# Half pages for the last rows of experts, in a two-layer graph network with routed experts

## The chip, the cores and the metric

The kernel runs on one core of a Trainium2 chip. The metric is device time in microseconds for one execution, on that core. Its engines are TensorE (PE; PEld is its weight load), VectorE (DVE), ScalarE (ACT), GpSimd (POOL) and SyncE (SP). Transfers are issued from the queues of SP, ACT and POOL and run on 16 DMA engines.

## What is computed

128 graphs of 64 nodes, so N = 8192 rows of D = 256 values in fp32, go through two layers. Each layer is a graph step and then a mixture of experts; both add to x.

```python
# layer 0
x = x + gnn0(layernorm(x), adj)      # (adj @ x + eps * x) W1, rmsnorm, silu, W2
h = layernorm(x)
logits = h @ gate_w.T                # 64 experts
top, idx = top_k(logits, 6)          # softmax over the 6
mix = sum_k softmax(top)[k] * (h @ lattice_weights[idx[k]])   # 256 x 256 each
x = x + layernorm(h + mix @ out_w.T + out_b)
# layer 1
h = layernorm(layernorm(x))          # the second one has gamma and beta
x = x + relu-conv(h, adj, W_rel, W_root)
h = layernorm(x)
top, idx = top_k(h @ Wg + bg, 2)     # 8 experts, softmax over the 2
x = x + sum_k softmax(top)[k] * (relu(h @ W1[e] + b1[e]) @ W2[e] + b2[e])
```

A row so goes to 6 of 64 experts in layer 0 (49152 copies) and to 2 of 8 in layer 1 (16384 copies). Which experts is known only while the kernel runs.

## The kernel before

**Routing.** Both layers use the class Router. Row blocks of 256 are scored; each chosen copy gets a place in a table in DRAM (`r0x`, `r1x`), in its expert's part of it, and POOL writes it there with one indirect DMA per 128 copies (`send`, L408). A copy carries its destination and its gate value in two extra columns (W = D + 2). Behind the last copy of each expert, ACT's queue writes a filler page whose destination lies outside the answers (`fill_end`, L519 to L525).

An expert's copies are read back in pages: 128 rows in layer 0 (pg = P), 256 in layer 1 (pg = 2 P). Its last page may be partly filled; in layer 0 each of 64 experts can have one. `page_table` (L432 to L517), a long row of small DVE operations at the end of the routing, orders all pages: first the full pages up to R per expert, then the other full ones, then the partly filled ones. For page number i the table `tab` gives the row where it begins (row 0 of `tab`) and its expert (row 1). SP loads the row number into a register before it fetches a page, PE loads the expert's number before its matmuls. The number of pages that the data needs, `total_pages`, is compared with a static number by `needed`: pages beyond it stand inside `tc.If` and run only if needed.

**Layer 0's experts.** The weights of all 64 experts lie in SBUF (`lat`). 12 early pages, one for each of 12 experts, are taken first (`fetch_early`, `flip_early`, `apply_early`). Then pages run in pairs: `fetch` (SP, L554, one DMA a page into `px`, 22 buffers of a pair), `flip` (four PE transposes into PSUM, one ACT copy to `pxT`), `apply` (two matmuls a page, L1068, then a DVE scaling by the gate value, L1072), and `reply`: POOL's indirect DMA that scatters 128 answers into `r0y` (L415). `staggered` writes the order out: at step s, the fetch of pair s + 12, `apply` of pair s, and the flip of pair s + 3 (s + 2 for the first four).

**The fused pass.** It runs over 32 blocks: `load_y` (L1197) fetches the six answers of each row, `mixture` sums them with transposes, `out_proj`, layer norm, then layer 1's graph step with `w_rel` and `w_root`, and layer 1's routing. Answers for the first 6 blocks (READY) are known to come from pages in the front of the order, so these loads need not wait for the last replies; later ones do. The small weights are asked for on ACT's queue as the pass begins (L1182 to L1186). The order of engines' instructions is written by hand here too.

**Layer 1's experts.** Four first pages (FIRST, numbers -4 to -1; three of them are fetched within the fused pass) and then pages 0 to 64. `fetch1` brings a page's rows into `px` (4 buffers), the expert's first weights into `pw` (3 buffers, 514 KB) and its bias into `pb`; `flip1` transposes, `up` makes the hidden values (16 matmul records over 256 columns, ACT's relu), `down` multiplies by the second weights (16 records), `share` makes the gate value, and `answer` (L1169 to L1175) adds the bias and scales on DVE into `py_s` (2 buffers) and has POOL add the rows to the output in DRAM: `add` (L423 to L430), one accumulating indirect DMA per 128 rows, two a page. The adds of one page need not wait for each other, but those of the next page wait until these have landed, as two pages can hold the same row.

`answer(-4)` and `answer(-3)` stand in DVE's order behind layer 1's `page_table` (L1486 to L1493).

Of the kernel before, what the change touches and what calls it, by code (L numbers as in the profile page):

```python
# [106 lines left out]
class Router:  # L107
# [15 lines left out]
    def __init__(self, tc, pool, small, dram, n, D, E, K, T, pg, S, epoch, name, R, total=None, like=None):  # L123
# [4 lines left out]
        self.pages = K * n // pg + E - 1  # L128

        self.likely_pages = K * n // pg + E // 2 + max(E // 8, 1)  # L130
# [301 lines left out]
    def page_table(self, scratch):  # L432
# [28 lines left out]
        v.scalar_tensor_tensor(part, full, -float(pg), cnt, op0=ALU.mult, op1=ALU.add)  # L461
        v.tensor_scalar(part, part, 0.0, None, op0=ALU.is_gt)
# [5 lines left out]
        self.total_pages = self.pool.tile([P, 1], I32, name=n + "total")  # L468
        if self.seen is None:
            v.tensor_copy(self.total_pages, cum[:, V - 1:V])  # L470
        else:

            far = small([1], "far")
            v.scalar_tensor_tensor(cnt, first, -float(pg), self.seen, op0=ALU.mult, op1=ALU.add)
            if self.taken is not None:
                v.scalar_tensor_tensor(cnt, self.taken, -float(pg), cnt, op0=ALU.mult, op1=ALU.add)
            v.tensor_reduce(far, cnt, op=ALU.max, axis=AX.X)
            v.tensor_scalar(far, far, 0.0, float(self.pages), op0=ALU.is_gt, op1=ALU.mult)
            v.tensor_tensor(self.total_pages, far, cum[:, V - 1:V], op=ALU.max)
# [4 lines left out]
        self.tab = self.pool.tile([P, 2, 4], I32, name=n + "tab")  # L484
# [32 lines left out]
        v.tensor_scalar(self.tab[:, 1, :], exp, float(E - 1), None, op0=ALU.min)  # L517

# [8 lines left out]
    def load(self, what, i, engine):  # L527

        top = (self.spare, self.E - 1)[what]
        _, v = self.nc.values_load_multi_w_load_instructions(  # L530
            self.tab[i // 4:i // 4 + 1, what, :], engines=[engine], min_val=0, max_val=top,
            skip_runtime_bounds_check_because="the page table holds no other values for any counts")
        return v
# [14 lines left out]
    def fetch_first(self, row, out):  # L548

        d = self.nc.sync.dma_start(out=out, in_=self.table[ds(row, self.pg), :].rearrange("(t p) d -> p t d", p=P))  # L550
        self.tc.declare_no_dep(d.ins, group=self.name + "late", reason="full pages get no rows")

# [16 lines left out]
def two_layer_gnn_moe_kernel(ctx: ExitStack, tc: tile.TileContext, a: dict, out: bass.AP):  # L569
# [16 lines left out]
    READY = 6  # L586
    FOLD = 2
# [88 lines left out]
    with tc.tile_pool(name="c0", bufs=1) as c0, \  # L676
# [201 lines left out]
        r0 = Router(tc, const, small, dram, N, D, E0, K0, T, P, 14 * P, 4, "r0", 3)  # L878
        r1 = Router(tc, const, small, dram, N, D, E1, 2, T, 2 * P, N, 4, "r1", 1, total=out, like=r0)
# [136 lines left out]
    with tc.tile_pool(name="wx0", bufs=3, reuse_waits="tile") as wx, \  # L1016
# [3 lines left out]
        pairs = [dict() for _ in range(npair)]  # L1020
# [16 lines left out]
        def fetch(j):  # L1037
            Q = pairs[j]
            Q["px"] = px = wx.tile([P, 2, W], F32, name="px", bufs=22)
            for q in range(2):  # L1040
                i = 2 * j + q
                if i % 4 == 0:
                    regs["row"] = r0.load(0, i, ENG.SP)
                if i < r0.pages:
                    r0.fetch(i, regs["row"][i % 4], px[:, q:q + 1, :])

        def flip(j):
            Q = pairs[j]
            pt = pt_pool.tile([P, KD, C], F32, name="pt")
            n = min(2, r0.pages - 2 * j)  # L1050
# [3 lines left out]
            Q["xT"] = xT = ring.pop() if ring else wx.tile([P, KD, C], F32, name="pxT", bufs=5)  # L1054
            nc.scalar.copy(xT[:, :, :n * P], pt[:, :, :n * P])  # L1055

        def apply(j):
# [3 lines left out]
            if j % 2 == 0:  # L1061
                regs["e"] = r0.load(1, 2 * j, ENG.PE)
            py = py_pool.tile([P, 2, D], F32, name="py")
            px, xT = Q["px"], Q["xT"]
            n = min(2, r0.pages - 2 * j)
            for q in range(n):
                for k in range(KD):
                    nc.tensor.matmul(py[:, q, :], lhsT=xT[:, k, ts(q, P)],  # L1068
                                     rhs=lat[:, ds(regs["e"][(2 * j + q) % 4], 1), k, :].rearrange("p o d -> p (o d)"),
                                     start=(k == 0), stop=(k == KD - 1))  # L1070
            for q in range(n):
# [5 lines left out]
                  (-2, lambda j: flip(j) if j < 4 else None), (-3, lambda j: flip(j) if j >= 4 else None))  # L1077
        likely = (r0.likely_pages - EARLY + 3) // 4 * 2

        mean_pages = (K0 * N // P + E0 // 2 - EARLY) // 4 * 2  # L1080
        staggered(mean_pages, (*stages, (0, load_vectors)))
        wait = const.tile([1, 4], F32, name="wait")
        with tc.If(r0.needed(2 * mean_pages)):
            staggered(likely, stages, mean_pages)
            with tc.If(r0.needed(2 * likely)):
                staggered(npair, stages, likely)
# [11 lines left out]
    FIRST = 4  # L1098
    pages = {i: dict() for i in range(-FIRST, r1.pages)}
    regs = {}  # L1100

    likely = r1.likely_pages - FIRST

# [7 lines left out]
    def fetch1(i):  # L1111
        Q = pages[i]
        Q["x"] = x = wx.tile([P, 2, W], F32, name="px", bufs=4)
# [6 lines left out]
        if i % 4 == 0 or i == likely:  # L1120
            regs["row"], regs["esp"] = r1.load(0, i, ENG.SP), r1.load(1, i, ENG.SP)
        r1.fetch(i, regs["row"][i % 4], x)
        load1(i, regs["esp"][i % 4])


    def flip1(i):
        Q = pages[i]
        pt = Q["pt"](0)
        ops.transpose(pt, Q["x"])
        Q["xT"] = xT = wx.tile([P, KD, PG], F32, name="pxT")  # L1130
        nc.scalar.copy(xT, pt)

    def up(i, lo=0, hi=KF):
        Q = pages[i]
        w = Q["w"]
# [3 lines left out]
        for c0 in range(lo, hi, Q["group"]):  # L1139
            group = range(c0, c0 + Q["group"])  # L1140
            ph = [Q["ph"](c) for c in group]
            for c in group:
                for k in range(KD):
                    nc.tensor.matmul(ph[c - c0], lhsT=w[:, k * F1 + c * P:k * F1 + (c + 1) * P],  # L1144
                                     rhs=Q["xT"][:, k, :], start=(k == 0), stop=(k == KD - 1))
            for c in group:
                nc.scalar.activation(hid[:, c, :], ph[c - c0], AF.Relu, bias=w[:, KD * F1 + c:KD * F1 + c + 1],  # L1147
                                     scale=1.0)

    def down(i, e, tiles=(0, 1)):  # L1150
        Q = pages[i]
        if 0 in tiles:
# [8 lines left out]
    def share(i):  # L1161

        Q = pages[i]
        Q["p"] = p = wx.tile([P, 2], F32, name="p")
        nc.scalar.activation(p, Q["x"][:, :, D + 1], AF.Exp)  # L1165
# [3 lines left out]
    def answer(i):  # L1169
        Q = pages[i]  # L1170
        y, p = wx.tile([P, 2, D], F32, name="py_s"), Q["p"]
        nc.vector.tensor_add(y, Q["py"], Q["b2"].unsqueeze(1).to_broadcast([P, 2, D]))  # L1172
        for t in range(2):
# [3 lines left out]
    with tc.tile_pool(name="c3", bufs=1, reuse_waits="tile") as c3, \  # L1177
# [6 lines left out]
        w_rel = load_matrix(c3, "L1_gnn_W_rel")  # L1184
        w_root = load_matrix(c3, "L1_gnn_W_root")
# [7 lines left out]
        def load_y(b):  # L1193
            B = blocks[b]
            B["y"] = y = work.tile([P, T, K0, D], F32, name="y", bufs=3)
            for t in range(T):
                d = nc.sync.dma_start(out=y[:, t],  # L1197
                                      in_=r0.answer[ts(b * T + t, P * K0), :].rearrange("(p k) d -> p k d", k=K0))
                if b < READY:
                    tc.declare_no_dep(d.ins, group="r0last", reason="in the first pages, or waited for above")  # L1200

# [212 lines left out]
        for i in (-4, -3, -2):  # L1414
# [3 lines left out]
            (-2, load3),  # L1418
            (-4, load_y),
# [76 lines left out]
    with tc.tile_pool(name="pt4", bufs=2, space=PSUM, reuse_waits="tile") as pt_pool, \  # L1496
# [7 lines left out]
        def finish(i):  # L1504
            if 0 <= i < E1:
                r1.fill_end(i)
            if i >= 0 and (i % 4 == 0 or i == likely):
                regs["e"] = r1.load(1, i, ENG.PE)
            share(i)
            down(i, regs["e"][i % 4] if i >= 0 else i + FIRST)  # L1510
# [10 lines left out]
        stages = (-2, fetch), (0, then(flip1)), (1, finish), (0, then(up))  # L1521
        staggered(likely, stages, -2)
        with tc.If(r1.needed(likely)):
            staggered(r1.pages, stages, likely)
# [32 lines left out]
```

## Time and profile before

| What | us |
|---|---|
| median of 3 runs (1998.88 to 2004.12) | 1999.45 |
| the profiled execution | 2002.07 |
| its span, first to last instruction | 2000.2 |
| PE busy | 1879.9 (94%) |
| POOL busy | 1160.2 (58%) |
| DVE busy | 1150.2 (58%) |
| ACT busy | 1010.0 (50%) |

The page of the profile gives the busy time of each engine, then the span in 40 slices of 50 us with the busy share in tenths, the granted clock of PE (PEclk), and the DMA share. Groups of instructions follow: line, engine, operation, what is written and read, count, then busy time, the mean of one in ns, the idle time before them and what ended it. A matmul in fp32 shows as two records. The trace can also be asked for the busy time in a stretch, for waits (who waited for whom: total, times, longest), for the timeline of an engine (start, length, what), and for the chain of work that ended last. A line number can be that of a helper: L415 is every reply, L425 every add.

### The profile page before, as it was taken

What the parts mean: (1) busy time and instruction counts of PE and PEld (TensorE: products, weight loads), DVE (VectorE), ACT (ScalarE), POOL (GpSimd) and SP (SyncE); (2) the same over time, 40 slices, a digit from 0 to 9 for tenths busy, and PEclk for the clock granted to TensorE, in tenths of its full rate; (3) what the DMA queues carried; (4) which work ended last, traced back from release to release, by engine and by line L of the source; (5) the groups of instructions that cost most, each with busy time, mean ns of one, the idle gap of its engine ahead of it and who ended that gap; (6) DMA issues with size and microseconds to landing.
All of it is one profiled execution on the core that took longest, in us unless ns stands there. A gap on an engine that the chain in (4) does not pass through costs nothing. (4 is left out here: it accounts for less than half of the span.)

```text
span 2000.2 us, 36067 instructions
## 1 busy us (share of the span) xinstructions
PE 1879.9 (94%) x10004; PEld 1628.7 (81%) x10004; DVE 1150.2 (58%) x4231; ACT 1010.0 (50%) x2033; POOL 1160.2 (58%) x1134
## 2 busy tenths in 40 slices
PE   7999999999947899999999799999999999999996
PEld 6888888888836778888777688888788888888885
DVE  5899999999974333444333489999842222222221
ACT  5888888888821222222222366666733333333331
POOL 1377777777777777777777744444453434444343
PEclk9999999999978999999999999999999999999998
DMA  4234555554468988666665799787247666666674
GB/s 127 72 127 137 161 163 163 161 163 132 153 220 271 288 259 255 208 206 207 212 205 167 283 380 336 263 282 257 96 131 184 160 150 152 160 163 161 152 167 88
DMA packets 265148, 381.07 MB, mean 191 GB/s; under 512 B 55000, under 2 KB 218984, under 8 KB 264944
## 3 DMA queue, kind: packets, MB, share of 16 engines
q1 hardware_dynamic: 185744, 230.88, 38.8%
q0 software_dynamic: 64416, 136.14, 22.5%
q10 hardware_dynamic: 14784, 11.64, 1.8%
q8 instruction: 90, 1.47, 0.3%
q14 instruction: 114, 0.93, 0.2%
HBM read 214.45 MB, written 168.25 MB: 191 GB/s over the span
## 5 line engine op out<-in xcount | busy, mean ns | idle before, releaser
L408 POOL DMA_INDIRECT r0x<-xs,r0row x384 | 386.9, 1008 | 216.9 <-ACT lat L784 114.3
L415 POOL DMA_INDIRECT r0y<-px x404 | 392.8, 972 | 124.6 <-DMA r0y<-px 49.4
L1068 PE MATMUL py<-lat,pxT 128*128 x1616 | 389.6, 385 | 17.1 <-ACT pxT L1055 13.8
L425 POOL DMA_INDIRECT out_x<-py_s,px x138 | 214.5, 1554 | 303.6 <-DMA out_x<-py_s,px 256.5
L1072 DVE TENSOR_SCALAR px<-py,px 128x256 f32<-128x256 f32 x404 | 177.0, 479 | 310.3 <-PE py L1068 304.6
L1068 PEld LDWEIGHTS py<-lat,pxT 128*128 128x128 f32 x1616 | 294.0, 192 | 57.0 <-ACT pxT L1055 18.2
L1055 ACT COPY pxT<-pt 128x512 f32<-128x512 f32 x202 | 117.9, 585 | 369.4 <-PE pt L1053 251.6
L1147 ACT ACTIVATE phid<-ph,pw 128x256 f32<-128x256 f32 x264 | 125.0, 473 | 312.0 <-PE ph L1144 232.6
L1157 PE MATMUL py<-fw,phid 128*128 (+1 forms) x1072 | 243.2, 380 | 1.3 <-issue 0.6
L795 PE MATMUL ps<-lat 128*128 128x256 f32 x1024 | 238.9, 382 | 0.0
L1144 PE MATMUL ph<-pxT,pw 128*128 128x256 f32 x1056 | 238.7, 379 | 0.0
L759 PE MATMUL ph<-lat 128*128 128x256 f32 x1024 | 232.5, 386 | 3.2 <-DVE lat L782 2.0
L408 POOL DMA_INDIRECT r1x<-xs,r1row x128 | 135.6, 1059 | 170.6 <-DVE bn_mv L59 45.0
L1144 PEld LDWEIGHTS ph<-pxT,pw 128*128 128x128 f32 x1056 | 200.6, 190 | 27.3
L1157 PEld LDWEIGHTS py<-fw,phid 128*128 128x128 f32 x1072 | 198.5, 190 | 27.7 <-issue 2.3
L759 PEld LDWEIGHTS ph<-lat 128*128 128x128 f32 x1024 | 195.4, 193 | 29.9 <-issue 2.4
L795 PEld LDWEIGHTS ps<-lat 128*128 128x128 f32 x1024 | 193.3, 191 | 28.1
L1172 DVE TENSOR_TENSOR py_s<-py,pb 128x512 f32<-128x512 f32 x67 | 46.3, 691 | 173.3 <-PE py L1157 101.4
L1053 PE MATMUL pt<-ident,px 128*128 128x128 f32 x808 | 126.7, 277 | 13.1 <-DMA px<-r0x 12.8
L1166 DVE TENSOR_SCALAR p<-p 128x2 f32<-128x2 f32 x69 | 11.6, 169 | 213.3 <-ACT p L1165 213.3
L1053 PEld LDWEIGHTS pt<-ident,px 128*128 128x128 f32 x808 | 101.2, 143 | 40.2 <-DMA px<-r0x 10.8
L782 DVE SCALAR_TENSOR_TENSOR lat<-ph,c_L_gnn_b,rms 128x256 f32<-128x256 f32 x256 | 111.9, 476 | 23.2 <-ACT rms L72 23.2
(327 smaller groups left out, 2945.5 us busy)
## 6 DMA issues: line engine op xcount, KB each, us to landing
px<-r0x SPq DMA_DIRECT2D x404, 129.0 KB
y<-r0y SPq DMA_DIRECT2D x64, 768.0 KB
pw<-in_L_ffn_W1b SPq DMA_DIRECT2D x69, 514.0 KB
px<-r1x SPq DMA_DIRECT2D x69, 258.0 KB
x<-x SPq DMA_DIRECT2D x64, 256.0 KB
pb<-in_L_ffn_b SPq DMA_DIRECT2D x69, 128.0 KB
r0x<-r0filler ACTq DMA_DIRECT2D x64, 129.0 KB
lat<-in_x SPq DMA_DIRECT2D x32, 256.0 KB
```

The source lines that it names most:

```text
L408: i = self.nc.gpsimd.indirect_dma_start(out=self.table[:, :], out_offset=bass.IndirectOffsetOnAxis(ap=row[:, t, k:k + 1], axis=0), in_=xs[ ...
L415: d = self.nc.gpsimd.indirect_dma_start(out=self.answer[:, :], out_offset=bass.IndirectOffsetOnAxis(ap=x[:, self.D:self.D + 1].bitcast(I32 ...
L425: i, d = f"{self.name}add{i}", self.nc.gpsimd.indirect_dma_start(out=self.total[:, :], out_offset=bass.IndirectOffsetOnAxis(ap=x[:, self.D ...
L759: nc.tensor.matmul(ph[:, c, :], lhsT=w1[:, k, ts(2 * j + c, P)], rhs=B["aggT"][:, k, :], start=(k == 0), stop=(k == KD - 1))
L795: nc.tensor.matmul(B["po"][:, t, :], lhsT=B["hT"][:, c, ts(t, P)], rhs=w2[:, c, :], start=False, stop=(t == T - 1 and c == KH - 1))
L1053: nc.tensor.transpose(pt[:, k, ts(q, P)], Q["px"][:, q, ts(k, P)], ident)
L1055: nc.scalar.copy(xT[:, :, :n * P], pt[:, :, :n * P])
L1068: nc.tensor.matmul(py[:, q, :], lhsT=xT[:, k, ts(q, P)], rhs=lat[:, ds(regs["e"][(2 * j + q) % 4], 1), k, :].rearrange("p o d -> p (o d)") ...
L1072: nc.vector.tensor_scalar(px[:, q, :D], py[:, q, :], px[:, q, D + 1:D + 2], None, op0=ALU.mult)
L1144: nc.tensor.matmul(ph[c - c0], lhsT=w[:, k * F1 + c * P:k * F1 + (c + 1) * P], rhs=Q["xT"][:, k, :], start=(k == 0), stop=(k == KD - 1))
L1147: nc.scalar.activation(hid[:, c, :], ph[c - c0], AF.Relu, bias=w[:, KD * F1 + c:KD * F1 + c + 1], scale=1.0)
L1157: nc.tensor.matmul(py[:, t, :], lhsT=Q["hid"][:, c, ts(t, P)], rhs=fw2[:, ds(e, 1), c, :].rearrange("p o d -> p (o d)"), start=(c == 0), s ...
```

## The change

**In the router.** Layer 0's expert with 1 to 64 rows in its last page, and layer 1's with 1 to 128, no longer gets a page of its own in the order: its last rows become a half page. `page_table` counts a remainder as a page only above pg / 2, makes a second list of the experts with a half page, and adds two rows to `tab` (first row and expert of each half page). `total_pages` becomes the larger of the page count and of the half count shifted, so that one comparison covers both limits. The static numbers change: layer 0 foresees 376 pages and 28 halves outside the conditionals (404 pages before), layer 1 foresees pages up to number 57 and 7 halves (up to 64 before).

**Layer 0.** Four half pages make a pair: two tiles of 128 rows, each with the last rows of two experts. They are fetched with four DMAs of 64 rows. A tile's transposed rows are written into a `pxT` buffer of their own as first half, zeros, second half, and each tile then takes two matmuls for each of the two depth tiles, one per expert, summed in PSUM. A tile has one scaling and one reply, as before. The half pairs come last in the order: 188 pairs, then 7 half pairs, where 202 pairs stood.

**Layer 1.** A half page is an item of 128 rows: half the transposes, `up` over 128 columns, one tile of `down`, one add; its weights are loaded as for a page. Five halves are put in ahead of pages 16, 24, 32, 40 and 48, two come last. `px` has 6 buffers instead of 4 and `py_s` 3 instead of 2.

**Fused pass.** `w_rel` and `w_root` are loaded from SP's queue, behind the first block's answers and ahead of the second's, instead of from ACT's queue at the beginning.

```diff
-        self.pages = K * n // pg + E - 1
+        self.halves = halves
+        self.pages = K * n // pg + (E // 2 if halves else E - 1)
+        self.likely_pages, self.likely_halves = likely
...
+        left = small([E], "left")
+        v.scalar_tensor_tensor(left, full, -float(pg), cnt, op0=ALU.mult, op1=ALU.add)
+        v.tensor_scalar(part, left, pg / 2.0 if self.halves else 0.0, None, op0=ALU.is_gt)
...
+            v.scalar_tensor_tensor(ends, left, 0.0, part, op0=ALU.is_gt, op1=ALU.subtract)
+            v.tensor_tensor_scan(upto, ends, self.zero[:, :E], 0.0, op0=ALU.add, op1=ALU.add)
+            v.scalar_tensor_tensor(count, upto[:, E - 1:E], float(self.likely_pages - self.likely_halves),
+                                   cum[:, V - 1:V], op0=ALU.add, op1=ALU.max)
...
+        if self.halves:
+            le = le[:, :, :E]
+            v.tensor_tensor(le, wide(upto, 1, E), wide(self.page, 2, E), op=ALU.is_le)
+            v.tensor_reduce(exp, le, op=ALU.add, axis=AX.X)
+            v.tensor_tensor(ate, wide(self.expert, 1, E), wide(exp, 2, E), op=ALU.is_equal)
+            v.tensor_sub(left, self.last, left)
+            v.tensor_scalar(left, left, float(self.spare), None, op0=ALU.subtract)
+            v.tensor_mul(le, ate, wide(left, 1, E))
+            v.tensor_reduce(row, le, op=ALU.add, axis=AX.X)
+            v.tensor_scalar(self.tab[:, 2, :], row, float(self.spare), None, op0=ALU.add)
+            v.tensor_scalar(self.tab[:, 3, :], exp, float(E - 1), None, op0=ALU.min)
...
+    def fetch_half(self, row, out):
+        n = self.pg // 2
+        self.nc.sync.dma_start(out=out, in_=self.table[ds(row, n), :].rearrange("(t p) d -> p t d", p=min(n, P)))
...
+            if j >= npair:
+                regs["row"] = r0.load(2, 4 * (j - npair), ENG.SP)
+                for i in range(4):
+                    q, h = i // 2, i % 2 * P // 2
+                    r0.fetch_half(regs["row"][i], px[h:h + P // 2, q:q + 1, :])
+                return
...
+            for q in range(n):
+                xT = wx.tile([P, KD, C], F32, name="pxT", bufs=5)
+                Q["xT"].append(xT)
+                nc.vector.memset(xT[:, :, P // 2:P + P // 2], 0.0)
+                for h in (0, 1):
+                    nc.scalar.copy(xT[:, :, 3 * h * P // 2:3 * h * P // 2 + P // 2],
+                                   pt[:, :, q * P + h * P // 2:q * P + h * P // 2 + P // 2])
...
+                for h in range(parts):
+                    e = regs["e"][2 * q + h if parts == 2 else (2 * j + q) % 4]
+                    for k in range(KD):
+                        nc.tensor.matmul(py[:, q, :], lhsT=xT[q][:, k, ts(h, P)] if parts == 2 else xT[:, k, ts(q, P)],
...
+        run((*range(usual), *range(npair, ends)), (0, load_vectors))
...
-        Q["x"] = x = wx.tile([P, 2, W], F32, name="px", bufs=4)
+        Q["x"] = x = wx.tile([P, 2, W], F32, name="px", bufs=6)
...
-        y, p = wx.tile([P, 2, D], F32, name="py_s"), Q["p"]
+        y, p, n = wx.tile([P, 2, D], F32, name="py_s", bufs=3), Q["p"], Q["n"]
...
-        for t in range(2):
+        for t in range(n):
...
+        def load_weights(b):
+            if b == 0:
+                for t, v in ((w_rel, "L1_gnn_W_rel"), (w_root, "L1_gnn_W_root")):
+                    nc.sync.dma_start(out=t, in_=a[v].rearrange("(k p) f -> p k f", p=P))
...
+        order = list(range(-2, likely))
+        for i in range(r1.pages, some - 2):
+            order.insert(order.index(E1 * (i - r1.pages + 2)), i)
+        run((*order, *range(some - 2, some)))
```

## The prediction

> **What bounds the kernel now.** I read the page's slices first (where is PE not full?), then busy time by stretch, then the waits of SP and POOL, then the timeline at the stages' ends. Five stages: layer 0's graph part (0 to 550 us), routing (550 to 620), layer 0's experts (620 to 1101), the fused pass (1107 to 1470), layer 1's experts (to the end). The change edits the third and fifth, and a little around them.
>
> ```profile
> PE   7999999999947899999999799999999999999996
> ...
> POOL 1377777777777777777777744444453434444343
> ...
> L415 POOL DMA_INDIRECT r0y<-px x404 | 392.8, 972 | 124.6 <-DMA r0y<-px 49.4
> ...
> L425 POOL DMA_INDIRECT out_x<-py_s,px x138 | 214.5, 1554 | 303.6 <-DMA out_x<-py_s,px 256.5
> ```
> PE looks full nearly everywhere, but POOL's two rows decide. L415 sends a page's answers: 0.97 us each with 0.30 between, so 1.27 a page, 2.55 a pair, without a pause from 615 us to 1147. L425 adds a page to the output in two DMAs of 1.55 us; 256.5 us of its waits are for an earlier add to land.
>
> SP's waits from 960 to 1101 us (total, times, longest), and two windows of line L1068 alone (stretch, length, PE busy with its records, PEld busy with its, clock, DMA share, GB/s):
>
> ```profile
> SPq L554 <- DMA r0y<-px: 58.9, 41, 2.6
> ```
> ```profile
> 900.00:960.00 60.00, 52.61 (x224) 40.02 (x222) 1.00 0.69 211
> 960.00:1101.00 141.00, 108.34 (x456) 82.23 (x456) 1.00 0.63 191
> ```
> SP's fetches wait for replies, as 22 px buffers are held until then. 224 records in 60 us are 28 pairs, 2.14 each; 456 in 141 us are 57, 2.47 each. So up to 960 us PE runs ahead at its own pace (four transposes 0.44, eight matmul records 1.73); from then on it is held near POOL's 2.55. The timeline at the end of the stage:
>
> ```profile
> 1096.08 5.35 PE L1068 MATMUL py<-lat,pxT 128*128 x24
> ...
> 1102.07 2.56 SPq L1197 DMA_DIRECT2D y<-r0y  x4
> ...
> 1107.47 2.79 PE L1215 MATMUL ps<-ident,y 128*128 128x128 f32 x12 [6.05 <-DMA y<-r0y]
> ```
> The fused pass begins when PE ends, not POOL: its first loads leave 0.65 us after the last matmul, while POOL goes on until 1147. Then layer 1's last stage, in the chain of waits and in a window of all engines (PE, PEld, DVE, ACT, POOL):
>
> ```profile
> 1502.77 0.71 issue
> 1503.48 1.55 POOL out_x L425
> 1505.03 0.30 issue
> 1505.33 4.86 DMA out_x<-py_s,px
> ```
> ```profile
> 1475.00:1990.00 515.00, 495.05 (x2396) 428.86 (x2394) 116.08 (x340) 172.20 (x400) 214.09 (x138) 0.99 0.67 156
> ```
> The chain repeats these four lines page after page. A page's adds go out only when those of the page before have landed. From the first (1474.61) to the last page's (1986.32) are 511.7 us for 68 steps, 7.52 each; PE needs 0.44 + 3.46 + 3.45 = 7.35. Two limits nearly level, POOL's chain the slower: in 515 us PE idles 20.
>
> **Does the data fit the new static counts?** I counted the reference's choices from its inputs (no time in that). Layer 0: 349 full pages, 36 remainders over 64 rows, 27 of 1 to 64; less the 12 early pages, 373 whole pages of 376 foreseen, 27 halves of 28. Layer 1: 61 full, 1 remainder over 128, 7 below; less 4 early, 58 whole of 58 and 7 halves of 7. So both conditionals stay untaken, as now (400 of 404 and 65 of 65). The smallest gap between a chosen and a rejected logit is 1e-5 on a spread of 0.33; layer 1's nearest remainders are 118 (10 rows from counting as whole) and 13. The numbers hold.
>
> **The change, part by part.**
>
> *Layer 0, replies.* 202 pairs become 188 plus 7 half pairs: 404 replies to 390, POOL ends 14 x 1.27 = 17.8 us earlier. That is not on the path, as the pass starts at PE's end; its later loads, which do wait for the last reply (1149.94 in SP's timeline), come earlier too, without a stall to remove: PE is busy 274.9 of 275 us from 1150 on.
>
> *Layer 0, PE.* Pair 187's matmuls end at 1067.3, the last at 1101.4: the 14 pairs that go cost 34.1 us. The 7 half pairs that come have two matmuls for each old one, both over 256 columns: 16 records, 2 x 1.73 = 3.46, and 0.44 for four transposes. The first one's transposes stand before pair 187, so 7 x 3.46 + 6 x 0.44 = 26.9. **Gain 7.2 us**; PE itself limits here, as SP's fetches come every 2.55. Beside it:
>  - ACT copies four 128x128 pieces instead of one 128x512 (0.59). The nearest row, 128x256, is 0.47: at most 1.9 a pair, under PE's 3.9. DVE clears two 128x256 pieces; its 128x128 memset takes 0.17, so below 0.5 each, behind two 0.47 scalings. Hidden; with the cover gone, the first half pair waits 0 to 2 us.
>  - PE loads four registers for each half pair, now for every second pair. Even and odd pairs both start 2.17 apart around 880 us: 0, at most the 0.5 of its longest "issue" waits, 3 us in all.
>  - SP issues four 64-row fetches instead of two of 128. Its issues stand 0.6 apart: 2.4 us a pair, under 3.9. Here the Trainium skill speaks against the change: DMA: Bandwidth & Descriptors, Rules for kernel authors, says that two transfers to disjoint partition halves serialize and should be one. By its roughly 2 us fixed cost, two more in series delay the first half pair by 4, and the gain is 3.2. By the trace a fetch of 129 KB is followed by its transpose 1.4 to 3.5 us after issue, and pair 188's fetch (1060.1) is wanted at about 1065. I take 0.
>
> *Layer 0, page table.* 12 more DVE operations: five 128x256 at 0.43, five 64-wide at 0.15 to 0.3, two writes: 3.6 us. They delay the early scalings from 607.94 to 611.5. POOL's first reply leaves at 614.90, behind POOL's own sends, and SP's first fetch at 616.38, behind their landing: 0. With that cover gone, at most 3.6.
>
> *Fused pass' weights.* W_rel and W_root (256 KB each) leave ACT's queue for SP's, after the first y block and ahead of the second. The ramp is DMA-bound (share 0.94 from 1101 to 1125), so the first y lands up to 0.5 MB at 0.35 to 0.4 MB/us = 1.4 us sooner. But out_proj of block 0 stands in PE's order behind the second block's mixture, and the same bytes go ahead of that. Taken as 0, between -1.4 and +1.4 (SP's two extra issues 1.2).
>
> *Layer 1, start.* 12 more DVE operations at about 0.17 (the 49 there now run from 1466.15 to 1472.99, 0.14 each): 2.0 us, and these are on the path, since answer(-4) waits behind them on DVE and POOL's chain starts with it. **Loss 2.0.**
>
> *Layer 1, chain.* 69 whole pages become 62 and 7 halves. A half sends one DMA. No such step is in the trace, but its parts are. By the packets, a page's first add has its last packet 3.40 us after its issue ends (second add: 2.89), and POOL goes on 1.2 us after the last packet. So a half step is 1.55 + 3.40 + 1.2 = 6.15, against 7.55 for a page beside fetches. The last page's adds, with no fetch beside them, land in 1.8: then 4.55. The Trainium skill (the same page, Anatomy of one DMA) gives about 2.0 us plus bytes over 436 GB/s: 2.3 for 128 KB in place of my 4.6 for landing and waking, so a step of 3.85 and five times 2.3 = 11.5 us more gain. I take the row, since it contains the contention; both ends, 3.85 and 7.5, go into the range. Sum after: 60 x 7.55 + 2 x 6.6 + 5 x 6.15 + 4.55 + 3.35 (last issue and landing) = 504.9; before 511.7 + 5.2 = 516.9. **Gain 12.0.** PE, at 59 x 7.35 + 7 x 3.7 + 3.5 = 463, has room; a half costs it 0.22 + 1.73 + 1.73.
>
> *More buffers* (px 4 to 6, y 2 to 3) let PE run further ahead of the adds. As POOL waits for landings and not for PE, 0; bounds 0 to 5 of gain, if the steps above 9 us shrink.
>
> Sum: 7.2 - 2.0 + 12.0 = 17.2. The profiled execution took 2002.07 (span 2000.2), so 1984.9; it stands 2.6 above the median of the runs, 1999.45, which gives **1982**. 0.3%, about what can be told from no change, is 6 us.
>
> **Rivals.**
>  - *A half's add is as long as a page's* (7.5; landing, not issue, rules), and halves in layer 0 cost their cover: the chain gains 12.0 - 5 x 1.35 - 3 = 2, layer 0 gains 4, minus 2.0: 1995. For it: landings vary from 2.9 to 6.7 whatever the load. Against: the second issue with its gap is 1.85 of the step. 0.07.
>  - *Landing is short without a second DMA*, and two more buffers absorb the slow steps: 11.5 + 5 more, 1966. For it: 1.8 us in quiet. Against: half pages still load whole weights, so DMA is as busy. 0.14.
>  - *Slower: an overrun.* One remainder more than foreseen, an eighth half or a 59th page in layer 1, opens the conditional: 10 whole pages and a half, 10 x 7.55 + 6.15 = 82 us, so 2064; in layer 0, beyond 376 pages or 28 halves, 4 pairs and 9 half pairs, 4 x 2.55 + 9 x 3.9 = 45, so 2027. Layer 1 has no spare page at all; yet my counts fit exactly. 0.03.
>  - *It doesn't do what it says*: buffers and weight order move nothing. That is already in my sum.
>  - Small unforeseen losses that leave it within 6 us: 0.03.
>
> **How the numbers follow.** The sum above has 0.73, its own range 1974 to 1991. 1970 to 1992 takes in half of the short-landing case. Faster by over 0.3% (below 1993.5): 0.73 + 0.14 + 0.04 of the first rival = 0.91; within: 0.05; slower: 0.04.
>
> **What would show it.** Right: 390 replies and 131 adds; the first load of y 6 to 8 us earlier; POOL's steps at halves near 6.2, others still 7.5; first add about 5 us earlier in the run, PE idle some 40 us in the last stage. Wrong: half steps of 7.5 or below 5; PE gaps between half pairs; PE full to the end with POOL waiting on DVE, which would mean that the chain wasn't the limit; a conditional's pages in the counts.

## The result, and the profile after

The kernel after takes 1982.38 us (median of 6 runs, 1981.85 to 1986.13), the kernel before 1999.16 in the same session (6 runs, 1996.23 to 2004.12). The ratio is 0.9918, 95% interval 0.9901 to 0.9935: about 17 us less, clear of 0.3%. The profiled execution took 1981.85 (span 1979.7, granted clock 0.972; before 2002.07, 2000.2 and 0.980). One reservation for what follows: seven of the experiments (b0 to b3, d1, d2, f1) ran on other chips, where layer 0 took some 300 us longer for every kernel and ScalarE and VectorE began instructions up to 11 us late; they are compared with the kernel before on those chips, and read for absolute times only behind layer 0, where they agree with the other profiles.

The counts are those foreseen. From the profile after, two rows of the slices and the two groups on POOL:

```profile
PE   7999999999956898999989899999999999999992
...
POOL 1377777777677677777777634444444434444433
...
L415 POOL DMA_INDIRECT r0y<-px x390 | 378.9, 972 | 123.1 <-DMA r0y<-px 50.0
...
L425 POOL DMA_INDIRECT out_x<-py_s,px x131 | 203.4, 1553 | 294.1 <-DMA out_x<-py_s,px 189.3
```
390 replies, 131 adds, no page of a conditional; the wait for landed adds fell from 256.5 to 189.3 us, though for seven long waits after (32.7 us), six of them behind half pages' adds, the profile names no releaser.

At the end of layer 0, the experts' matmuls (L1115) in windows before and behind the last whole pair (stretch, length, PE busy, PEld busy, clock, DMA share, GB/s), SP's wait from 960 us on, and the timeline where the stage ends:

```profile
960.00:1069.00 109.00, 84.61 (x355) 63.70 (x353) 1.00 0.66 205
1069.00:1097.00 28.00, 25.25 (x113) 20.82 (x112) 1.00 0.40 125
```
```profile
SPq L579 <- DMA r0y<-px: 45.5, 39, 2.6
```
```profile
1093.64 2.54 PE L1115 MATMUL py<-lat,pxT 128*128 x11
...
1096.35 0.83 SPq L1261 DMA_DIRECT2D y<-r0y  x2
...
1101.26 1.09 PE L1284 MATMUL ps<-ident,y 128*128 128x128 f32 x4 [5.08 <-DMA y<-r0y]
```
Seven half pairs follow the last whole one without a gap: from 1069.0 to 1096.2. The fused pass' first load leaves 0.2 us later, at 1096.35; before it was 1102.07.

The last stage as a whole (PE, PEld, DVE, ACT, POOL), and POOL's adds around the first half page (each line: start, length, idle before it):

```profile
1475.00:1970.00 495.00, 465.16 (x2323) 409.12 (x2321) 114.25 (x336) 167.18 (x400) 203.41 (x131) 0.98 0.67 159
```
```profile
1618.35 1.55 POOL L425 DMA_INDIRECT out_x<-py_s,px  x1 [0.30 <-issue]
1625.68 1.55 POOL L425 DMA_INDIRECT out_x<-py_s,px  x1 [5.79 <-DMA out_x<-py_s,px]
1632.36 1.55 POOL L425 DMA_INDIRECT out_x<-py_s,px  x1 [5.13 <-issue]
1634.21 1.55 POOL L425 DMA_INDIRECT out_x<-py_s,px  x1 [0.30 <-issue]
```
The add at 1625.68 is the half page's: alone, and the next page's goes out 6.67 us behind it. From the first add to that of the last page now lie 490.9 us, before 511.7 (this stretch is called the add chain below). Page steps average 7.30 us (7.53 before), the five half steps beside fetches 6.79, the one without them 4.49. The total is as predicted, but page steps were not to change: 62 of them with 0.23 less each are 14 us that the prediction did not have. Part of them lies between single executions: e4 below has layer 1 as before, and 7.45. The experiments ask where the rest comes from, and what ate as much elsewhere.

### The profile page after: what moved, and what is told of

Same layout as the page of the kernel before. It is cut to its first block, busy times and chain, and to the rows that moved or that the text cites. A ratio compares the mean times of both kernels' runs of the same rounds, so it can differ in the third digit from the quotient of the medians.

```text
span 1979.7 us, 35753 instructions
## 1 busy us (share of the span) xinstructions
PE 1852.6 (94%) x9906; PEld 1611.9 (81%) x9906; DVE 1150.0 (58%) x4248; ACT 1001.9 (51%) x2047; POOL 1134.9 (57%) x1113
## 5 line engine op out<-in xcount | busy, mean ns | idle before, releaser
L415 POOL DMA_INDIRECT r0y<-px x390 | 378.9, 972 | 123.1 <-DMA r0y<-px 50.0
L1115 PE MATMUL py<-lat,pxT 128*128 x1616 | 386.4, 383 | 19.3 <-ACT pxT L1089 15.9
L425 POOL DMA_INDIRECT out_x<-py_s,px x131 | 203.4, 1553 | 294.1 <-DMA out_x<-py_s,px 189.3
L1115 PEld LDWEIGHTS py<-lat,pxT 128*128 128x128 f32 x1616 | 293.1, 191 | 60.2 <-ACT pxT L1089 21.8
L1089 ACT COPY pxT<-pt 128x512 f32<-128x512 f32 x188 | 109.7, 585 | 346.1 <-PE pt L1086 232.3
L1209 ACT ACTIVATE phid<-ph,pw 128x256 f32<-128x256 f32 (+1 forms) x264 | 122.0, 462 | 294.6 <-issue 146.9
L1220 PE MATMUL py<-fw,phid 128*128 (+1 forms) x1016 | 230.7, 380 | 1.8 <-issue 1.0
L1206 PE MATMUL ph<-pxT,pw 128*128 128x256 f32 (+1 forms) x1056 | 227.2, 368 | 0.6 <-DMA pw<-in_L_ffn_W1b 0.6
L1206 PEld LDWEIGHTS ph<-pxT,pw 128*128 128x128 f32 x1056 | 192.8, 190 | 26.0 <-issue 1.4
L1237 DVE TENSOR_TENSOR py_s<-py,pb 128x512 f32<-128x512 f32 (+1 forms) x67 | 44.5, 664 | 290.7 <-DMA out_x<-py_s,px 232.7
L1220 PEld LDWEIGHTS py<-fw,phid 128*128 128x128 f32 x1016 | 187.9, 190 | 25.3 <-issue 1.6
L1086 PEld LDWEIGHTS pt<-ident,px 128*128 128x128 f32 x780 | 97.3, 142 | 35.1 <-issue 7.0
L788 ACT ACTIVATE lat<-ph,c_L_gnn_b 128x256 f32<-128x256 f32 x256 | 103.5, 470 | 32.6 <-PE ph L785 28.3
```

What stands on the lines that cost most here:

```text
L415: d = self.nc.gpsimd.indirect_dma_start(out=self.answer[:, :], out_offset=bass.IndirectOffsetOnAxis(ap=x[:, self.D:self.D + 1].bitcast(I32 ...
L425: i, d = f"{self.name}add{i}", self.nc.gpsimd.indirect_dma_start(out=self.total[:, :], out_offset=bass.IndirectOffsetOnAxis(ap=x[:, self.D ...
L1086: nc.tensor.transpose(pt[:, k, ts(q, P)], Q["px"][:, q, ts(k, P)], ident)
L1115: nc.tensor.matmul(py[:, q, :], lhsT=xT[q][:, k, ts(h, P)] if parts == 2 else xT[:, k, ts(q, P)], rhs=lat[:, ds(e, 1), k, :].rearrange("p ...
L1206: nc.tensor.matmul(ph[c - c0][:, :m], lhsT=w[:, k * F1 + c * P:k * F1 + (c + 1) * P], rhs=Q["xT"][:, k, :m], start=(k == 0), stop=(k == KD ...
L1209: nc.scalar.activation(hid[:, c, :m], ph[c - c0][:, :m], AF.Relu, bias=w[:, KD * F1 + c:KD * F1 + c + 1], scale=1.0)
```

## The experiments

**One part at a time.** First the buffers taken out of the kernel after, and put alone into the kernel before.

```diff
 # e1: the kernel after
-        Q["x"] = x = wx.tile([P, 2, W], F32, name="px", bufs=6)
+        Q["x"] = x = wx.tile([P, 2, W], F32, name="px", bufs=4)
-        y, p, n = wx.tile([P, 2, D], F32, name="py_s", bufs=3), Q["p"], Q["n"]
+        y, p, n = wx.tile([P, 2, D], F32, name="py_s", bufs=2), Q["p"], Q["n"]
 # e2: the kernel before
-        Q["x"] = x = wx.tile([P, 2, W], F32, name="px", bufs=4)
+        Q["x"] = x = wx.tile([P, 2, W], F32, name="px", bufs=6)
-        y, p = wx.tile([P, 2, D], F32, name="py_s"), Q["p"]
+        y, p = wx.tile([P, 2, D], F32, name="py_s", bufs=3), Q["p"]
```


> The kernel after, with layer 1's px buffers back from 6 to 4 and py_s from 3 to 2. Theory (the two added buffers are what shortens layer 1's whole-page steps from 7.52 to 7.30 us): page steps go back to about 7.5, and the run takes 62 x 0.22 = 14 us more, about 1996. Rival A (the half pages between the whole ones, or chance, shorten them): page steps stay at 7.3 and the time at about 1982. Prediction on record (buffers cost and bring nothing): 1982.

Measured: ratio to the kernel before 0.9929 (0.9913 to 0.9945), 1987.92 beside 2003.1 for the kernel before on this chip. Page steps 7.41, add chain 495.1. By the ratios that is 2 us above the kernel after, with overlapping intervals, where 14 were expected.

> The kernel before, with px 6 and py_s 3 in layer 1 and nothing else of the change. Theory (buffers shorten page steps): 68 steps of 7.3, so 15 us less, about 1984. Rival A (half pages do it, or chance): 7.5 each, about 1999. If buffers help only beside halves, because halves vary the demand: 1999 here, and about 1996 for the kernel after with few buffers.

Measured: 0.9965 (0.9953 to 0.9978), 1996.28, so 7 us less. Page steps 7.33, chain 498.6. The buffers do shorten page steps: without halves 7.33, against 7.53 and 7.45 in two profiles; with halves 7.24 to 7.36 in the eight profiles that have both buffers and this order of pages, against 7.41 in e1. Half of the expected 15 us comes out without halves, less with them.

Then each layer's part alone:

```diff
 # e3: layer 0 as before
-r0 = Router(..., "r0", 3, ((K0 * N // P - EARLY) // 4 * 4 + 4, E0 // 2 - 4), True)
+r0 = Router(..., "r0", 3, ((K0 * N // P + E0 // 2 - EARLY) // 4 * 4, 0), False)
 # e4: layer 1 as before, px 4, py_s 2
-                    (N // P - E1 // 4 - FIRST, E1 - 1), True, total=out, like=r0)
+                    (N // P + E1 // 2 + 1 - FIRST, 0), False, total=out, like=r0)
 # both: w_rel, w_root by load_matrix on ACT's queue, no load_weights
```


> Layer 1's part alone, with its buffers: layer 0 has its 404 whole pages and no list of halves, the fused pass' weights come on ACT's queue. Theory: what layer 0 brought is 5 us and the weights' order 0, so this is 5 us above the kernel after, about 1987. If the granted clock's two drops in the fused pass (at 1433 and 1457 us of the profiled run after, some 4 us) come with layer 0's shift, it is only 1 us above, about 1983. If layer 0 brings the 7.2 of the prediction: 1990.

> Layer 0's part alone: layer 1 has its 65 whole pages with 4 px and 2 py_s buffers, weights on ACT's queue. Theory: 7.2 less 1.9 that the longer page table passes on: 5.3 us below the kernel before, about 1994; layer 0's last matmul about 5 us earlier, the first of the experts' matmuls 1.9 later. By the prediction 7.2 below: 1992. If the clock's drops belong to this shift, they show at about 1433 us here too, and the gain is 1 to 2 us: 1998.

Measured: e3 0.9929 (0.9915 to 0.9944), 14 us less than before; e4 0.9960 (0.9946 to 0.9974), 8 us less. Together that is 22, and the kernel with both has 16 to 17: the intervals, of 3 us either way for each ratio, just about meet. What e4's profile says of layer 0 is firmer. Four profiles with layer 0 as before (before, e2, e3, and c1 below) and three with half pairs (after, e1, e4), in us of the span:

| | as before | half pairs |
|---|---|---|
| page table's last row written | 607.4 to 608.5, mean 608.1 | 610.7, 611.9, 613.1; mean 611.9 |
| first fetch of an experts' page | 615.8 to 617.3, mean 616.55 | 617.95, 619.2, 620.2; mean 619.1 |
| last matmul behind the first fetch | 485.0 to 487.8, mean 486.2 | 478.2 to 479.9, mean 479.3 |

The experts themselves take 7.0 us less; 2.6 are lost ahead of them. How they are lost is seen around the table's end. First e3 (the table's second row on DVE, SP's load of the last 1 MB of the experts' weights, POOL's last send, SP's first fetch, then SP's wait before it), then the same for the kernel after:

```profile
607.05 0.34 DVE L526 TENSOR_SCALAR r0tab<-lat 128x4 int32<-128x4 f32 x1
...
607.43 0.39 SPq L996 DMA_DIRECT2D lat<-in_L_ffn_lattice_weights  x1
...
612.81 0.96 POOL L408 DMA_INDIRECT r0x<-xs,r0row  x1 [0.30 <-issue]
...
615.78 4.84 SPq L579 DMA_DIRECT2D px<-r0x  x8
...
SPq L579 <- DMA r0x<-xs,r0row: 7.1, 1, 7.1
```
```profile
610.41 0.26 DVE L537 TENSOR_SCALAR r0tab<-lat 128x4 int32<-128x4 f32 x1
...
610.71 0.39 SPq L996 DMA_DIRECT2D lat<-in_L_ffn_lattice_weights  x1
...
612.27 0.97 POOL L408 DMA_INDIRECT r0x<-xs,r0row  x1 [0.30 <-issue]
...
617.95 2.91 SPq L579 DMA_DIRECT2D px<-r0x  x5
...
SPq L579 <- DMA r0x<-xs,r0row: 5.9, 1, 5.9
```
The fetch waits for the landing of POOL's last send: in all seven profiles it leaves 0.12 us behind it. The send itself did not go out later (its issue ended at 613.78 to 614.85 without the list, at 613.24 to 614.44 with it), but it landed 4.6 to 5.6 us behind its issue with the list, in place of 1.7 to 2.3. What shifts with the table is SP's load of 1 MB, issued 0.05 us behind the table's last row. While it moves, POOL's queue stands. The transfers from 608.7 to 612.2 in e3, and from 612.0 to 615.6 in the kernel after (a queue's packets, MB and share of the 16 DMA engines, then what was issued in that time), are all of SP's queue, q1:

```profile
q1 hardware_dynamic: 845, 0.87, 86.8%
...
r0x<-xs,r0row POOLq DMA_INDIRECT x3
```
```profile
q1 hardware_dynamic: 858, 0.88, 92.5%
...
r0y<-early POOLq DMA_INDIRECT x2
r0x<-xs,r0row POOLq DMA_INDIRECT x1
```
So a longer table means a later load, and a later load means later landings. That the load holds POOL's packets back is read from their order in the seven profiles; no run moved the load alone. VectorE's scalings of the early pages also begin when the table is done, but they are no better explanation: in the profile of before POOL's queue stood from 611.6 to 612.4 too, when VectorE was idle.

**Which buffer?**

```diff
 # c1: the kernel before
-        Q["x"] = x = wx.tile([P, 2, W], F32, name="px", bufs=4)
+        Q["x"] = x = wx.tile([P, 2, W], F32, name="px", bufs=6)
```


> The kernel before, with px 6 in layer 1 but py_s left at 2. The kernel before with both changed had 7.33 us page steps and an add chain of 500.4 us, against 7.53 and 513.6 (508.6 in the second profile of the same layer 1 code), and its answers lay ready 8 to 13 us ahead of their adds, in place of 5 to 8. Theory (the shallow py_s buffer couples TensorE's page of 7.35 us to each landing; the third lets it run a page further ahead): px alone leaves the chain at 509 to 514 and the lead at 5 to 8. Rival (px buffers let the fetches leave at a better moment of the add step): the chain is at 500, the share of pages whose weights are asked for before the add falls in line with the run with both.

Measured: 0.9959 (0.9945 to 0.9973), 8 us less; page steps 7.33, chain 498.3, the same as with both. The answers' lead stayed at 6.9 us (median; 6.6 before, 11.2 with both), so the third py_s buffer lets TensorE run a page further ahead and brings nothing in itself. That theory fell. What six px buffers change is seen in a window of the last stage, before and then c1, and in c1's chain of waits there (that of before, adds and landings, stands in the prediction):

```profile
1480.00:1960.00 480.00, 469.38 (x2273) 406.57 (x2272) 108.91 (x317) 163.54 (x378) 197.19 (x127) 1.00 0.68 162
```
```profile
1480.00:1960.00 480.00, 480.00 (x2354) 422.83 (x2353) 118.79 (x331) 169.35 (x392) 203.09 (x131) 1.00 0.71 165
```
```profile
1504.70 3.45 PE ph L1144 x16
1508.15 0.44 PE pt L89 x4
1508.59 3.46 PE py L1157 x16
1512.04 3.45 PE ph L1144 x16
```
TensorE is busy 480.00 of 480 us, and the chain that ended last is here one of matmuls: 0.44 + 3.46 + 3.45 = 7.35 a page, with adds that come every 7.33. In c1 it stays one up to some 1885 us and is one of adds from there on; in e2 matmuls lead to the last pages. POOL's chain has become just short enough for TensorE to bound the stage. How the buffers shorten it is partly seen. Fetches still leave on a landing, in all kernels; a page's weights are asked for 1.07 us behind it (median), in place of 1.19, and more often before the next add is issued: 47 of 64 steps in c1 and 42 of 64 in e2, against 30 of 65 before and 41 of 65 in e4. In each of these profiles steps of the one kind land faster than those of the other (in c1 2.63 us and 3.08 behind the last add's issue). That an earlier request causes the faster landing is argued, not shown: e4 has the share without the gain. What fits it is that an add's packets, like the sends' above, stand while SP's loads move: the half page's add in the kernel after went out from 1625.68 to 1627.23, and the transfers from 1625.0 to 1629.2 are these:

```profile
q1 hardware_dynamic: 391, 0.70, 62.7%
...
pw<-in_L_ffn_W1b SPq DMA_DIRECT2D x1, 514.0 KB
...
out_x<-py_s,px POOLq DMA_INDIRECT x1
```

**The chain's start and order in layer 1.** The kernel after, unchanged, and two changes of it:

> The kernel after, unchanged, on the same chip as the three that follow. Theory (the two buffers are worth 6 us): the ratio to the kernel before stays at 0.992, 2 to 6 us below the kernel after with few buffers (which stood at 0.9929). Its clock shows a drop to 0.5 somewhere between 1430 and 1460 us here too, since the kernel before with two more buffers, whose fused pass is untouched, had one as well.

```diff
 # b1
-        r1.page_table(work.tile([P, 512], F32, name="scratch", bufs=1))
         share(-4)
         answer(-4)
+        r1.page_table(work.tile([P, 512], F32, name="scratch", bufs=1))
```


> The kernel after, with the first early page's answer ahead of layer 1's page table in VectorE's order. Theory (POOL's chain of adds sets the end, from its first add on; the table is on its path): the first add goes out behind the last send, at about 1471.4 in place of 1476.1, and everything to the end moves by 4.7 us: 1978 beside 1982. Rival (TensorE sets the end, or the first pages' fetches, which are 1.5 us later): 0 or up to 2 us worse.

```diff
 # b2
-        for i in range(r1.pages, some - 2):
-            order.insert(order.index(E1 * (i - r1.pages + 2)), i)
-        run((*order, *range(some - 2, some)))
+        run((*order, *range(r1.pages, some)))
```


> The kernel after, with layer 1's seven half pages all behind the 58 whole ones. Theory (a half step is long only for the transfers beside it): the halves at the end have 4.5 us steps in place of 6.7, 5 x 2.2 = 11 us less; as no half page then gives TensorE a lead between whole ones, these come at its 7.35 in place of 7.27, 62 x 0.08 = 5 us more: 6 us less in all, 1976 beside 1982. Rival (contention is the half's own, or TensorE was the real limit between the halves): 1982 to 1986.

Measured: ratios 0.9960 (0.9923 to 0.9997), 0.9933 (0.9909 to 0.9958) and 0.9935 (0.9905 to 0.9965), too wide on this chip to part them. The profiles do, counted from the last block's convolution, ahead of which the three do not differ:

| us behind the last block's convolution | after | b0 | b1 | b2 |
|---|---|---|---|---|
| first add | 25.8 | 26.3 | 22.2 | 27.0 |
| last matmul | 495.1 | 494.9 | 494.6 | 499.3 |
| end of the span | 529.4 | 529.4 | 529.1 | 529.4 |

b1's first add goes out 4 us sooner, right behind the last send, and nothing comes of it:

```profile
1792.13 1.62 POOL L425 DMA_INDIRECT out_x<-py_s,px  x1 [0.30 <-DVE scratch L458]
1794.05 1.58 POOL L425 DMA_INDIRECT out_x<-py_s,px  x1 [0.30 <-issue]
1802.19 1.58 POOL L425 DMA_INDIRECT out_x<-py_s,px  x1 [6.56 <-DVE py_s L1239]
```
The second page's adds wait for their answer (VectorE at L1239), which comes no earlier; the first two steps are 10.1 and 10.6 us, and the lead is gone. In b2 the last three half steps take 4.5 us, as expected, but the whole pages take 7.40 and the end is where it was. (The other profiles with this layer 1 end 529.6 to 530.8 us behind that convolution; only e3's does so after 523.2, in the fastest of its six runs, 8 us below their median; why is not explained.) Between its first add and its last matmul, the kernel after leaves TensorE 5.3 us idle of 469 (before 10.6 of 506). With both limits that near, shortening one of them alone gives nothing: theory and sizes of b1 and b2 were wrong, the rival (TensorE) right.

**Layer 0's list and order.**

```diff
 # b3: upto and the list's rows of r0.tab in a function of their own, over another scratch
         staggered(EARLY // 2, ((-2, flip_early), (0, apply_early)))
+        r0.half_list(et.tile([P, 11 * E0 + 8], F32, name="halves", bufs=1), left)
 # d1
-        run((*range(usual), *range(npair, ends)), (0, load_vectors))
+        mixed = list(range(usual))
+        for n, j in enumerate(range(npair, ends)):
+            mixed.insert(mixed.index(104 + 8 * n), j)
+        run(mixed, (0, load_vectors))
 # d2, f1: both
```


> The kernel after, with layer 0's list of half pages made behind the early pages' scalings instead of ahead of them (12 VectorE operations moved, 3 added). Theory (the first fetch of the experts' pages waits for the last early scaling, which waits for the table): the first fetch is back at about 616.4, layer 0's last matmul ends some 3 us earlier (about 1095.4 beside a mean of 1098.4 for the three profiles with the list in its old place), the time 3 us less, 1979. Rival (the fetch waits for the sends' landing, as the prediction has it, and 1.6 us are chance): no change.

Measured: 0.9901 (0.9862 to 0.9940), 2293.11 beside 2305.14 for b0 in the same session. On this chip the table came over 20 us behind the sends, and the fetch hung on it directly. DVE and SP in b0, then in b3:

```profile
811.53 0.16 DVE L537 TENSOR_SCALAR r0tab<-lat 128x4 int32<-128x4 f32 x1
...
812.73 2.17 SPq L579 DMA_DIRECT2D px<-r0x  x4
```
```profile
766.49 0.16 DVE L526 TENSOR_SCALAR r0tab<-lat 128x4 int32<-128x4 f32 x1
...
767.70 46.85 SPq L600 DMA_DIRECT2D px<-r0x  x44
...
778.60 0.16 DVE L558 TENSOR_SCALAR r0tab<-halves 128x4 int32<-128x4 f32 x1
```
With the list behind the scalings, the fetch follows the table's second row by 1 us and is out 11 us before the list is done; in b0 the second row was there at 808.9, 2.8 us before the list. That the list held up the fetch is thereby shown for this chip, where the sends had long landed and the fetch hung on the table alone. It did not hang on the last early scaling, as the theory had it: in both kernels the fetch leaves 6 to 8 us before that ends. Of the 12 us in the medians it explains about 3; the rest is this chip's spread (b0's runs lie between 2282 and 2338).

> The kernel after, with layer 0's seven half pairs not behind the 188 whole ones but one each ahead of pairs 104, 112, ... 152. Theory (from about 960 us on TensorE only follows POOL's replies, as many pairs ahead as the 22 px buffers let it; a half pair costs TensorE 3.9 us and POOL 2.55, so seven of them at the end eat up that lead, and in the middle, where TensorE runs faster than POOL, they cost nothing): POOL's last reply stays, TensorE's last matmul of layer 0 lies 46 us ahead of it again, as in the kernel before, in place of 34: about 11 us less, ratio to the kernel before 0.986, 1971 beside 1982. Rival (TensorE's own work, not POOL, sets the stage's end): the order moves nothing, 0.992.

> The kernel before this one, with layer 0's list of half pages made behind the early pages' scalings as well. Theory (the list held up the first fetch by 2.8 us): the first fetch 2.8 us earlier. But if POOL's replies set the stage's end, and these go out without a pause from the early ones on, only what they gain counts: the first reply waits for the early scalings behind the list, though behind POOL's last sends too, so 0 to 2 us less than the kernel before this one. Rival (the fetch's delay passes through to the end): 3 us less.

> The same kernel as the last one (half pairs ahead of pairs 104 to 152, list of half pages behind the early scalings), once more, since layer 0 took 300 us longer on the chip of the last runs, with ScalarE and VectorE starting late and POOL's replies not behind TensorE there, so that the theory could not show itself. Theory as before: where POOL's replies run on 34 us behind TensorE at the end of layer 0 (1130.6 against 1096.2 in the profile after), the half pairs in the middle give TensorE that lead back: last matmul at about 1085, last reply at about 1130, first fetch at 616.4; ratio to the kernel before 0.986 against 0.9918 for the kernel after. Rival (TensorE's own work sets the stage's end): last matmul at about 1093 by the earlier fetch alone, 0.990.

Measured: 0.9912 (0.9868 to 0.9955), 0.9902 (0.9873 to 0.9931), 0.9904 (0.9876 to 0.9932). Nothing can be said of the half pairs' place: on these chips TensorE waited for ScalarE's copies (in b0 80.8 us in 33 waits), and POOL's last reply ended 3 to 12 us behind the last matmul, not 34, so there was no lead to win back. What 34 us of replies behind the last matmul are worth on the first chip stays open. The three runs with the list moved (b3, d2, f1) stand at 0.990, those without it at 0.991 to 0.996: no single pair is parted by its intervals, but none points the other way. As a version that beats both kernels, the kernel after with the list behind the scalings (b3) is the best candidate; its time on the first chip was not measured.

## Why the prediction was right, and where it was not

It gave 1982 with 17.2 us of gain; measured were 1982.4 and 16.8. The mechanism of the main terms was right. Some terms were not, and they cancelled; that the total is right to 0.4 us is luck:

- **Layer 0, PE: -7.2.** Right: 7.0 over seven profiles from the first fetch on. Seven half pairs took 27.2 us (predicted 26.9), at 3.9 each, without gaps for ScalarE's four copies, VectorE's clears or register loads (in e1 and e4 the first half pair waited 0.4 and 0.5 us; predicted 0 to 2). The rule of the Trainium skill (DMA: Bandwidth & Descriptors, Rules for kernel authors) that two transfers to disjoint partition halves serialize, by which 4 us were at stake, showed no cost here (the 2 us behind these 4 stand on that page for transfers that POOL issues, and these are SP's): the first half pair's four fetches left from 1061.06 to 1063.13, and its matmuls began at 1069.57.
- **Layer 0, page table: 0, "behind POOL's own sends" and "behind their landing".** This step failed. The wait was named rightly: the first fetch does leave behind the landing of the sends. But the landing was taken not to move with the table, and it did. The table became 3.8 us longer (bound 3.6), the weights' load behind it and with it the landings came later, and 2.6 passed through. The trace of before had the signs: the load issued at 608.26, behind the table, and not a packet of POOL's queue from 609.5 to 613.0. On another chip, where the sends had landed, the fetch hung on the table itself.
- **Fused weights: 0.** Right: the first convolution follows layer 0's last matmul by 35.0 us on average with either queue (34.6 to 35.8 over five profiles with ACT's, 34.9 and 35.1 with SP's).
- **Layer 1, start: +2.0.** The table is 1.8 us longer by the same profiles, measured from the last convolution, and the first add later, but b1 shows that this is not on the path. Of the signs named, the first add was to come some 5 us earlier in the run; it came 1.5 later, at 1476.13, as what lies between layer 0 and it took 6.8 us more.
- **Half pages: -12.0.** Right in size by the profiles where buffers are as before: from e4 to e1 the chain falls from 506.8 to 495.1, 11.7, with half steps of 6.22 (predicted 6.15, against 3.85 by the price of a transfer in Anatomy of one DMA on the same page of the Trainium skill) and 4.54 in the quiet (predicted 4.55). The same layer 1 took 511.7 in the profile of before, so the 11.7 are good to some 5; the medians of e4 and e1, on one chip, lie 7.1 apart, with the later start in that. With six px buffers half steps are 6.79; that they meet more of SP's loads there is not shown.
- **More buffers: 0, "as POOL waits for landings and not for PE".** Mis-sized. POOL does wait for landings, but landings got shorter: 7 us less in e2, 8 in c1, 8 to 13 in their chains of whole pages (498.6 and 498.3 against 506.8 and 511.7); beside halves 4 in the chain (490.9 against e1's 495.1) and 2 by the ratios, which do not part the two. The bound was 5. TensorE, which had room by the sum (463 us from the first add on), took 469.3, of which it was idle 5.3.
- **The clock,** which no step had: the profile of before has no drop behind the first blocks of the fused pass, that of after two. After a PE wait of 2.65 us, the same in both, the clock fell to half in one (the kernel before first, then the kernel after):

```profile
1439.28 2.02 PE L1308 MATMUL pz<-m_L_gnn_W_rel,hT 128*128 128x256 f32 x8 [2.65 <-ACT hT L1300]
```
```profile
1434.33 3.78 PE L1377 MATMUL pz<-m_rel,hT 128*128 128x256 f32 x8 [2.65 <-ACT hT L1369]
```
This is no effect of the change: e2, whose fused pass is that of before, shows the same 3.78 at 1442.50 behind the same 2.65, and of all 14 profiles only before and c1 have no drop there. On the chips where layer 0 is not slowed, the profiles with a drop take 352.9 to 354.2 us from layer 0's last matmul to the last convolution, the two without (before, c1) 351.0 and 351.5.

Between the two profiled executions the sum can be made exactly: the last matmul of layer 0 comes 5.2 us earlier, the way from there to the first add is 6.8 longer, the add chain 20.8 shorter and what follows it 1.3 shorter, which makes the 20.5 between the spans. The medians differ by 16.8, since the execution profiled before lies 2.9 above its median and that after 0.5 below. By the profiles of the experiments layer 0 brings 4.4, half pages some 12 and the buffers beside them 4. By the ratios, taken in turn (before, e4, e1, after), these are 8, 6 and 2, with some 4 us of doubt on each of the last two, where 7.2, 10.0 (12.0 less the later start) and 0 were predicted. With that doubt, and with chains of the same code that differ by 5 us, more is not settled.

## What to carry to other kernels

Where two engines' cycles lie within 3% of each other (here 7.52 of serial adds and 7.35 of matmuls), work out the floor of the second before counting what the first gives up, and look at its busy share in the stage afterwards: at 480 of 480 us there is nothing left to win on the other side. A buffer is not worth nothing because its consumer waits for something else; it also sets when transfers leave. And for work put ahead of a stage on one engine, list every instruction and every transfer that starts behind it and who waits for each: the wait that ends last can itself be moved, here by a load that another queue's landing stood behind.

## What the runs showed of the hardware

The granted clock fell to half at an idle gap of 2.65 us, at one place of the fused pass, in 12 of 14 profiles, for 3.4 or 6.8 us, and stayed full in two. By the Trainium skill (TensorE: Matmul & The Clock Gate, Part 1) it goes back after an idle window of about 3.4 us that runs free of the kernel. A gap of 2.65 us does not fill such a window, and was enough here; what decides in which execution it is enough is not shown. A half page's add into DRAM (one DMA, 128 KB) had its last packet 1.8 to 1.9 us behind the end of its issue without other traffic, and 3.2 to 4.4 beside a page's fetch (kernel after and e1). While a load of 1 MB on SP's queue moved, no packet of POOL's queue did for some 3.6 us, though POOL had issued (e3 and the kernel after, above). And two chips of one kind differed by 300 us in a stage full of short ScalarE and VectorE instructions, while the later stages agreed within 1%: 877.5 us from layer 0's last matmul to the end, against 883.5.
